# A selective-scan network on one core: two scan tiles per step in place of one

## Chip, core and metric

One core of a Trainium2 chip runs the whole program in one launch. The metric is the device time of that launch in microseconds (us). The engines are TensorE (PE, matmuls; PEld are its weight loads), VectorE (DVE), ScalarE (ACT), GpSimd (POOL) and SyncE (SP, which issues the DMAs here). Each engine works through its own queue in program order; semaphores make it wait for the others.

## What is computed

Four layers on four images of 64 x 64 positions (L = 4,096 tokens) and 96 channels. Layer 0 has a gated recurrence, layers 1 to 3 a convolution and a selective scan in four directions; each layer ends with a small quantised feed-forward part. The change is in the scan of layers 1 to 3. Cut to what matters, one of them is:

```python
xc = silu(depthwise_conv3x3(x @ in_proj) + conv_b)        # 192 channels
xs = [rows of xc, columns of xc, both flipped]            # 4 directions
dts, B, C = split(xs @ x_proj)                            # 6, 16 and 16 rows
delta = softplus(dts @ dt_proj + dt_bias)
dA = exp(delta[..., None] * A)                            # 16 states per channel
def step(h, t):
    h = dA_t * h + (delta_t * u_t)[..., None] * B_t       # the recurrence over L
    return h, einsum('bkdn,bkn->bkd', h, C_t)             # y: sum over the 16 states
y = scan(step) + D * xs
x = x + (layernorm(sum of the 4 directions of y) * silu(z)) @ out_proj
x = x + ffn(layernorm(x))
```

Everything around the recurrence (projections, convolution, norms, feed-forward) is the "side work" below.

## The kernel before

**Tiles.** The recurrence of one image and layer is cut into items: 2 flip directions (`d`) x 4 segments of T = 1,024 tokens x 3 chunks of 128 rows. A chunk holds 64 channels in row order and 64 in column order. An item has NS = 16 tiles, one for each state n, of 128 partitions x 1,024 tokens in float32. With 3 layers and 4 images there are 288 items and 4,608 tiles, numbered k = 16 q + n.

**What a tile costs.** Six helpers make a tile (lines 876 to 958):
- `c_rows(k)`: two DMAs on SP spread the state's row of C over the partitions into a buffer `c` (6 buffers).
- `decays(k)`: ACT makes `da = exp(delta * A_n)` (3 buffers).
- `b_rows(k)`: PE multiplies a selection matrix with the rows of B (`bs`, bfloat16 parts), two matmuls of 512 columns, into `bc` in PSUM. `wide()` (line 119) gives it one of 2 buffers of [128, 1024].
- `scan(k, beside)`: DVE multiplies `bc` by `du` (= delta * u) in place, the product; then `beside()` issues a portion of side work; then DVE runs `tensor_tensor_scan` over the 1,024 tokens into `h` (3 buffers), starting from the column `carry[:, n]`.
- `carry(k)`: ACT copies the last column of `h` into `carry` for the next segment. `times_c(k)`: POOL multiplies `h` by `c`, in place of `c`.
- `accumulate(k)`: PE adds the 16 tiles of an item up in PSUM (`acc`, one buffer of [128, 1024]) with eight 64 x 64 matmul instructions; the first tile of an item adds eight more for the skip term or the other direction's sum. `take` copies the full `acc` to SBUF on ACT and `store` sends it to DRAM in four DMAs.

**Order.** Nothing reorders the instructions of an engine: the class `InOrder` (line 68) chains every engine's instructions in the order in which the program text issues them, SP's DMAs too. So the loop over tiles (lines 990 to 1043) fixes all five queues. One turn k issues: `carry(k-1)`, `c_rows(k+2)`, `decays(k+2)`, `b_rows(k+1)`, `times_c(k-1)`, the product of k, side work, the scan of k, `accumulate(k-3)`. On DVE that is product, side work, scan, product, side work, scan and so on.

**Side work.** `beside()` advances generators by one `yield` each: `chain` prepares delta and du of the next item (`prepare_chunk`: two PE matmuls, ACT exponentials and logarithms, four POOL operations), `segment` the B and C rows of the next segment (`prepare_segment`), and `work()` steps a `Job` at a rate of 1.6 rounds a turn, which is the previous and the next image's norms, projections, convolution and feed-forward. Side work has 2 PSUM banks, counted by `bank`, `release` and `settle`. At n = 13 `beside` finishes the preparation of the next item. `logarithms()` issues ACT's collected logarithms at n = 11.

**PSUM.** 2 x 2 banks for `bc`, 2 for side work, 2 for `acc`: all 8 are used.

Of the kernel before, what the change touches and what calls it, by code (L numbers as in the profile page):

```python
# [15 lines left out]
ALU = mybir.AluOpType  # L16
# [5 lines left out]
NS = 16  # L22
# [3 lines left out]
T = 1024  # L26
# [73 lines left out]
def metaformer(ctx: ExitStack, tc: tile.TileContext, x, l0_ab, l0_rest, ssm, ffn, out):  # L100
# [10 lines left out]
    def sb(bufs, tag, shape, dtype=F32):  # L111
        return pools[bufs].tile(shape, dtype, tag=tag, name=tag)
# [19 lines left out]
    def settle():  # L132
        banks["free"] += banks["back"]
        banks["back"] = 0
# [38 lines left out]
    for n in range(NS):  # L173
        for k in range(2):
            at = NS * k + n
# [678 lines left out]
    def scans(stages, jobs, pac):  # L854


        items = [
            Item(im, layer, d, seg if d == 0 else NSEG - 1 - seg, chunk)
            for im, layer in stages
            for d in range(2)  # L860
            for seg in range(NSEG)
            for chunk in range(3)
        ]
        at = lambda q: items[q] if 0 <= q < len(items) else None
        sg = load_segment(items[0])
        for i in items[:3]:
            i.sg = sg
        drain(Chain(prepare_segment(items[0], sg), True))
        drain(Chain(prepare_chunk(items[0]), True))
        tiles = [(i, n) for i in items for n in range(NS)]  # L870
        last = len(tiles) - 1
        live = {}
        carries = {}
        per = 2 * NSEG * 3

        def start(i):
            if i.first:
                carries[i.chunk] = sb(2, f"carry{i.chunk}", [128, NS])
                pool.memset(carries[i.chunk], 0.0)
            i.carry = carries[i.chunk]  # L880

        def c_rows(k):
            i, n = tiles[k]
            c = live[k, "c"] = sb(6, "c", [128, T])
            for half in range(2):
                row = NS * half + n
                sp.dma_start(
                    out=c[64 * half : 64 * half + 64],
                    in_=i.sg.cs[row : row + 1, :].to_broadcast([64, T]),
                )  # L890

        def decays(k):
            i, n = tiles[k]
            da = live[k, "da"] = sb(3, "da", [128, T])
            at = (3 * i.d + i.chunk) * NS + n
            act.activation(da, i.delta, AF.Exp, scale=weights[i.layer].decay[:, at : at + 1])

        def b_rows(k):
            i, n = tiles[k]
            b = live[k, "b"] = wide()  # L900
            for half in range(2):
                cols = slice(half * MM, (half + 1) * MM)
                pe.matmul(
                    b[:, cols], sel[:, n, :], i.sg.bs[:, cols], start=True, stop=True
                )

        def scan(k, beside):
            i, n = tiles[k]
            da, b = live.pop((k, "da")), live.pop((k, "b"))
            dve.tensor_tensor(b, i.du, b, ALU.mult)  # L910
            beside()
            h = live[k, "h"] = sb(3, "h", [128, T])
            step = slice(None, None, -1 if i.d else 1)
            dve.tensor_tensor_scan(
                h[:, step],
                da[:, step],
                b[:, step],
                initial=i.carry[:, n : n + 1],
                op0=ALU.mult,
                op1=ALU.add,  # L920
            )

        def carry(k):
            i, n = tiles[k]
            if not i.last:
                end = 0 if i.d else T - 1
                act.copy(i.carry[:, n : n + 1], live[k, "h"][:, end : end + 1])

        def times_c(k):
            i, n = tiles[k]  # L930
            c = live[k, "c"]
            pool.tensor_tensor(c, live.pop((k, "h")), c, ALU.mult)

        def add_quarters(i, v, lhs, start, stop):

            for k in range(2):
                for j in range(2):
                    p = slice(64 * j, 64 * j + 64)
                    o = 64 * (j ^ k)
                    pe.matmul(  # L940
                        i.acc[o : o + 64, j * MM : (j + 1) * MM],
                        lhs[p],
                        v[p, k * MM : (k + 1) * MM],
                        start=start,
                        stop=stop,
                        tile_position=(64 * j, o),
                    )

        def accumulate(k):
            i, n = tiles[k]  # L950
            h = live.pop((k, "c"))
            if n == 0:
                i.acc = pac.tile([128, T], F32, tag="acc", name="acc")
                if i.d == 0:
                    add_quarters(i, i.sg.us[i.chunk], weights[i.layer].skip[:, i.chunk, :], True, False)
                else:
                    add_quarters(i, i.yf, stacked, True, False)
            add_quarters(i, h, stacked, False, n == NS - 1)

        def take(i):  # L960
            i.y = sb(2, "y", [128, T])
            act.copy(i.y, i.acc)

        def store(i):
            for j in range(2):
                for k in range(2):
                    o = 64 * (j ^ k)
                    t = i.seg * T + k * MM
                    sp.dma_start(
                        out=i.im.y[i.chunk, 64 * j : 64 * j + 64, t : t + MM],  # L970
                        in_=i.y[o : o + 64, j * MM : (j + 1) * MM],
                    )

        chain = segment = None
        start(items[0])
        c_rows(0)
        c_rows(1)
        decays(0)
        decays(1)
        b_rows(0)  # L980
        working = []

        def work():

            while working and working[0].done:
                working.pop(0)
            if working:
                working[0].step()

        for k in range(last + 5):  # L990
            q, n = divmod(k, NS)
            if k <= last:
                item = items[q]
                nxt = at(q + 1)
                if n == 0:
                    if q % per == 0:
                        item.im.y = dram.tile([3, 128, L], F32, tag="y", name="y")
                        working += jobs[q // per]
                    if item.chunk == 2:
                        drain(segment, work, lambda: nxt.sg.steps)  # L1000
                    chain = Chain(prepare_chunk(nxt), True) if nxt is not None else None
                if item.chunk == 1 and n == 4 and at(q + 2) is not None:
                    if q % per == per - 2:
                        for job in jobs[q // per][:1]:
                            while not job.done:
                                work()
                                settle()
                    segment = Chain(next_segment(items[q + 2 : q + 5]))
                if n == 8 and nxt is not None:
                    start(nxt)  # L1010
                if n == 8 and nxt is not None and nxt.d == 1:
                    nxt.yf = sb(2, "y", [128, T])
                    sp.dma_start(out=nxt.yf, in_=nxt.im.y[nxt.chunk, :, nxt.seg * T : (nxt.seg + 1) * T])
            def beside():
                pump(chain)
                pump(segment)
                if n == 13:
                    drain(chain, work)
                    if item.chunk == 2:
                        drain(segment, work)  # L1020
                work()

            full = items[(k - 4) // NS] if k >= 4 and (k - 4) % NS == NS - 1 else None
            if full is not None:
                take(full)
            if 0 <= k - 1 <= last:
                carry(k - 1)
            if k + 2 <= last:
                c_rows(k + 2)
                decays(k + 2)  # L1030
            if n == 11:
                logarithms()
            if k + 1 <= last:
                b_rows(k + 1)
            if 0 <= k - 1 <= last:
                times_c(k - 1)
            if k <= last:
                scan(k, beside)
            if full is not None:
                store(full)  # L1040
            if 0 <= k - 3 <= last:
                accumulate(k - 3)
            settle()
        while working:
            work()
            settle()
# [377 lines left out]
```

## Time and profile before

| | |
|---|---|
| median of 3 runs | 19,418.7 us (19,401.0 to 19,423.9) |
| span of the profiled execution | 19,402.3 us |
| layer 0 | 0 to about 1,800 us |
| scans of layers 1 to 3 | about 1,800 to 19,187 us |
| rest of the last image | 19,187 to 19,402 us |
| busy, whole span | DVE 17,697.8 us (91%), PE 15,935.0 (82%), POOL 15,479.3 (80%), ACT 12,105.6 (62%) |
| DMA | 3,192 MB, mean 165 GB/s, queue 1 busy 62.3% of 16 engines' span |

Almost every instruction is put down to line 78, the helper of `InOrder`, so that groups are told apart by the tiles that they write and read: `bc<-du,bc` on DVE is the product, `h<-da,carry,bc` the scan, `c<-h,c` on POOL is `times_c`, `bc<-bs,sel` on PE is `b_rows`, `acc<-c,twice` is `accumulate`. A matmul in float32 appears as two instructions. The granted clock is the share of its full speed that PE was allowed; the records show 1.0 and 0.5 only. A group's idle time is that of its engine just before its instructions, with the instruction that ended most of it.

In the 40 slices of the page VectorE is busy nine tenths or more from the fifth slice to the thirty-seventh:

```
PE   8998787787788788788788788788788787787887
DVE  6757999999999999999999999999999999999895
ACT  4544665665665665675665675665665665666665
POOL 3435888888888888888888888888888888888885
PEclk9998796786786797797797797797797797788775
```

### The profile page before, as it was taken

What the parts mean: (1) busy time and instruction counts of PE and PEld (TensorE: products, weight loads), DVE (VectorE), ACT (ScalarE), POOL (GpSimd) and SP (SyncE); (2) the same over time, 40 slices, a digit from 0 to 9 for tenths busy, and PEclk for the clock granted to TensorE, in tenths of its full rate; (3) what the DMA queues carried; (4) which work ended last, traced back from release to release, by engine and by line L of the source; (5) the groups of instructions that cost most, each with busy time, mean ns of one, the idle gap of its engine ahead of it and who ended that gap; (6) DMA issues with size and microseconds to landing.
All of it is one profiled execution on the core that took longest, in us unless ns stands there. A gap on an engine that the chain in (4) does not pass through costs nothing. (4 is left out here: it accounts for less than half of the span.)

```text
span 19402.3 us, 222370 instructions
## 1 busy us (share of the span) xinstructions
PE 15935.0 (82%) x69248; PEld 4652.0 (24%) x69248; DVE 17697.8 (91%) x13768; ACT 12105.6 (62%) x19150; POOL 15479.3 (80%) x10086
## 2 busy tenths in 40 slices
PE   8998787787788788788788788788788787787887
PEld 3332121121122222222222222222222222222323
DVE  6757999999999999999999999999999999999895
ACT  4544665665665665665675665665665665666665
POOL 3435888888888888888888888888888888888885
PEclk9998796786786797797797797797797797788775
DMA  2213666676676666666667676667676676676664
GB/s 53 50 46 87 166 187 172 167 191 168 167 190 173 173 183 182 172 183 181 172 187 183 172 186 178 170 185 185 170 191 177 170 192 175 171 193 170 168 180 115
DMA packets 1269866, 3192.20 MB, mean 165 GB/s; under 512 B 440336, under 2 KB 440560, under 8 KB 1262544
## 3 DMA queue, kind: packets, MB, share of 16 engines
q1 hardware_dynamic: 1268688, 3177.97, 62.3%
q8 instruction: 559, 9.16, 0.2%
q14 instruction: 619, 5.07, 0.1%
HBM read 2818.51 MB, written 308.28 MB: 161 GB/s over the span
## 5 line engine op out<-in xcount | busy, mean ns | idle before, releaser
L78 POOL TENSOR_TENSOR c<-h,c 128x1024 f32<-128x1024 f32 (+1 forms) x4992 | 11318.6, 2274 | 3241.4 <-DVE h L78 1326.1
L78 DVE TENSOR_TENSOR_SCAN h<-da,carry,bc 128x1024 f32<-128x1024 f32 x4608 | 10798.3, 2343 | 567.9 <-POOL c L78 63.3
L78 PE MATMUL acc<-c,twice 64*64 64x512 f32 x36864 | 6385.9, 770 | 39.2 <-POOL c L78 39.1
L78 ACT ACTIVATE da<-delta,decay 128x1024 f32<-128x1024 f32 x4608 | 5284.4, 1148 | 1425.8 <-DVE h L78 1414.0
L78 DVE TENSOR_TENSOR bc<-du,bc 128x1024 f32<-128x1024 f32 x4608 | 5569.1, 1209 | 287.4 <-PE bc L78 264.7
L78 PE MATMUL bc<-bs,sel 96*128 96x512 bf16 x9216 | 3486.1, 468 | 2663.6 <-DVE h L78 2562.1
L78 ACT COPY carry<-h 128x1 f32<-128x1 f32 x3456 | 649.0, 188 | 3121.5 <-DVE h L78 3117.1
L78 PEld LDWEIGHTS <-sel 96*128 96x128 bf16 x9216 | 561.9, 102 | 7786.2 <-DVE h L78 5970.8
L78 PEld LDWEIGHTS acc<-c,twice 64*64 64x64 f32 x36864 | 1148.5, 156 | 2882.6 <-issue 1988.2
L78 ACT ACT_TABLE_LOAD x1166 | 1496.0, 1283 | 36.8 <-DVE mv L78 20.2
L78 PE MATMUL conv<-pad,tap_lo 128*128 128x512 f32 x1728 | 919.9, 639 | 0.0
L78 PE MATMUL dt_proj<-rows,w 12*128 12x512 f32 x1152 | 846.8, 822 | 9.6 <-ACT delta L78 5.5
L78 ACT COPY y<-acc 128x1024 f32<-128x1024 f32 x288 | 291.5, 1012 | 822.6 <-PE acc L78 807.4
L78 PE MATMUL x_proj<-u,xp 128*108 128x512 f32 x1152 | 706.2, 731 | 31.4 <-ACT u L78 12.4
L78 POOL TENSOR_TENSOR delta<-delta,du 128x1024 f32<-128x1024 f32 x288 | 679.3, 2359 | 60.5 <-ACT du L78 58.9
L78 ACT ACTIVATE du<-e,ones 128x1024 f32<-128x1024 f32 x576 | 659.8, 1146 | 108.6 <-POOL delta L78 103.7
L78 POOL TENSOR_TENSOR e<-e,du 128x1024 f32<-128x1024 f32 x288 | 679.6, 2360 | 2.4 <-ACT du L78 2.4
L78 POOL TENSOR_TENSOR du<-delta,u 128x1024 f32<-128x1024 f32 x288 | 679.6, 2360 | 0.1
L78 ACT ACTIVATE c<-c,l_bias 128x512 f32<-128x512 f32 x384 | 263.4, 686 | 667.0 <-PE c L78 664.2
L78 POOL TENSOR_TENSOR delta<-delta,e 128x1024 f32<-128x1024 f32 x288 | 678.4, 2356 | 0.1
L78 PE MATMUL conv<-pad,tap_hi 128*128 128x512 f32 (+1 forms) x1152 | 609.0, 632 | 19.0 <-ACT u L78 16.7
L78 DVE TENSOR_TENSOR_SCAN h<-da,l_carry,bc 128x512 f32<-128x512 f32 x384 | 491.4, 1280 | 42.4 <-DVE bc L78 1.8
(149 smaller groups left out, 14606.8 us busy)
## 6 DMA issues: line engine op xcount, KB each, us to landing
c<-cs SPq DMA_DIRECT2D x9216, 256.0 KB, 4.2
u<-u SPq DMA_DIRECT2D x288, 512.0 KB, 6.7
y<-y SPq DMA_DIRECT2D x1152, 128.0 KB, 3.5
y<-y SPq DMA_DIRECT2D x144, 512.0 KB, 6.2
xr<-x SPq DMA_DIRECT2D x224, 192.0 KB, 5.0
u<-u SPq DMA_DIRECT2D x288, 128.0 KB, 3.8
pad<-y SPq DMA_DIRECT2D x288, 128.0 KB, 4.5
z<-zl SPq DMA_DIRECT2D x96, 256.0 KB, 4.4
```

The lines of the kernel that those rows point to most:

```text
L78: ins = f(*a, **k).ins
```

## The change

The loop takes two tiles a = 2j and b = 2j + 1 per step. `scan` is split into `times_b` (the product) and `scan`, and `beside` is called twice a step, with `settle` inside. The order of one step on each engine becomes:

- DVE: product a, side work, product b, scan a, side work, scan b.
- PE: accumulate a-4, accumulate b-4, side work, rows of a+2, side work, rows of b+2.
- ACT: decay of b, carry of a-2 and b-2, decay of a+2, side work twice; at step 1 of an item also `take` of the item before.
- POOL: `times_c` of b-2, side work twice, `times_c` of a.
- SP: `c_rows` of a+2 and b+2, each issued behind the accumulation that frees its buffer; side work's DMAs; `store`.

The instructions themselves, their number and their sizes stay, and so do the buffers. The reading of `live[k, "h"]` changes because `carry` now comes after `times_c` for tile a.

```diff
@@ -904,11 +904,14 @@
                     b[:, cols], sel[:, n, :], i.sg.bs[:, cols], start=True, stop=True
                 )
 
-        def scan(k, beside):
+        def times_b(k):
+            i, n = tiles[k]
+            b = live[k, "b"]
+            dve.tensor_tensor(b, i.du, b, ALU.mult)
+
+        def scan(k):
             i, n = tiles[k]
             da, b = live.pop((k, "da")), live.pop((k, "b"))
-            dve.tensor_tensor(b, i.du, b, ALU.mult)
-            beside()
             h = live[k, "h"] = sb(3, "h", [128, T])
             step = slice(None, None, -1 if i.d else 1)
             dve.tensor_tensor_scan(
@@ -929,7 +932,7 @@
         def times_c(k):
             i, n = tiles[k]
             c = live[k, "c"]
-            pool.tensor_tensor(c, live.pop((k, "h")), c, ALU.mult)
+            pool.tensor_tensor(c, live[k, "h"], c, ALU.mult)
 
         def add_quarters(i, v, lhs, start, stop):
 
@@ -973,11 +976,10 @@
 
         chain = segment = None
         start(items[0])
-        c_rows(0)
-        c_rows(1)
+        for k in range(2):
+            c_rows(k)
+            b_rows(k)
         decays(0)
-        decays(1)
-        b_rows(0)
         working = []
 
         def work():
@@ -987,31 +989,36 @@
             if working:
                 working[0].step()
 
-        for k in range(last + 5):
-            q, n = divmod(k, NS)
-            if k <= last:
+        half = NS // 2
+        for j in range(len(tiles) // 2 + 2):
+            q, m = divmod(j, half)
+            a, b = 2 * j, 2 * j + 1
+            on = b <= last
+            if on:
                 item = items[q]
                 nxt = at(q + 1)
-                if n == 0:
+                if m == 0:
                     if q % per == 0:
                         item.im.y = dram.tile([3, 128, L], F32, tag="y", name="y")
                         working += jobs[q // per]
                     if item.chunk == 2:
                         drain(segment, work, lambda: nxt.sg.steps)
                     chain = Chain(prepare_chunk(nxt), True) if nxt is not None else None
-                if item.chunk == 1 and n == 4 and at(q + 2) is not None:
+                if item.chunk == 1 and m == 2 and at(q + 2) is not None:
                     if q % per == per - 2:
                         for job in jobs[q // per][:1]:
                             while not job.done:
                                 work()
                                 settle()
                     segment = Chain(next_segment(items[q + 2 : q + 5]))
-                if n == 8 and nxt is not None:
+                if m == 4 and nxt is not None:
                     start(nxt)
-                if n == 8 and nxt is not None and nxt.d == 1:
-                    nxt.yf = sb(2, "y", [128, T])
-                    sp.dma_start(out=nxt.yf, in_=nxt.im.y[nxt.chunk, :, nxt.seg * T : (nxt.seg + 1) * T])
-            def beside():
+                    if nxt.d == 1:
+                        nxt.yf = sb(2, "y", [128, T])
+                        t = slice(nxt.seg * T, (nxt.seg + 1) * T)
+                        sp.dma_start(out=nxt.yf, in_=nxt.im.y[nxt.chunk, :, t])
+
+            def beside(n):
                 pump(chain)
                 pump(segment)
                 if n == 13:
@@ -1019,28 +1026,42 @@
                     if item.chunk == 2:
                         drain(segment, work)
                 work()
-
-            full = items[(k - 4) // NS] if k >= 4 and (k - 4) % NS == NS - 1 else None
-            if full is not None:
-                take(full)
-            if 0 <= k - 1 <= last:
-                carry(k - 1)
-            if k + 2 <= last:
-                c_rows(k + 2)
-                decays(k + 2)
-            if n == 11:
+                settle()
+
+            if on:
+                decays(b)
+            for k in (a - 2, b - 2):
+                if 0 <= k <= last:
+                    carry(k)
+            if a + 2 <= last:
+                decays(a + 2)
+            if m == 5:
                 logarithms()
-            if k + 1 <= last:
-                b_rows(k + 1)
-            if 0 <= k - 1 <= last:
-                times_c(k - 1)
-            if k <= last:
-                scan(k, beside)
-            if full is not None:
-                store(full)
-            if 0 <= k - 3 <= last:
-                accumulate(k - 3)
-            settle()
+            if 0 <= b - 2 <= last:
+                times_c(b - 2)
+                del live[a - 2, "h"], live[b - 2, "h"]
+            for k in (a - 4, b - 4):
+                if 0 <= k <= last:
+                    accumulate(k)
+                if k + 6 <= last:
+                    c_rows(k + 6)
+            if on:
+                times_b(a)
+            beside(2 * m)
+            if on:
+                times_b(b)
+                scan(a)
+            if a + 2 <= last:
+                b_rows(a + 2)
+            beside(2 * m + 1)
+            if on:
+                times_c(a)
+                scan(b)
+            if b + 2 <= last:
+                b_rows(b + 2)
+            if m == 1 and q >= 1:
+                take(items[q - 1])
+                store(items[q - 1])
         while working:
             work()
             settle()
```

## The prediction

> **What bounds the kernel now.** I read the page first, its groups of instructions before the rest. Columns: instruction, written tile, read tiles, count; busy us and mean ns of one; idle time before them and what ended it.
>
> ```profile
> L78 DVE TENSOR_TENSOR_SCAN h<-da,carry,bc 128x1024 f32<-128x1024 f32 x4608 | 10798.3, 2343 | 567.9 <-POOL c L78 63.3
> L78 PE MATMUL acc<-c,twice 64*64 64x512 f32 x36864 | 6385.9, 770 | 39.2 <-POOL c L78 39.1
> L78 DVE TENSOR_TENSOR bc<-du,bc 128x1024 f32<-128x1024 f32 x4608 | 5569.1, 1209 | 287.4 <-PE bc L78 264.7
> L78 PE MATMUL bc<-bs,sel 96*128 96x512 bf16 x9216 | 3486.1, 468 | 2663.6 <-DVE h L78 2562.1
> ```
>
> VectorE makes 4,608 products of 1.209 us and 4,608 scans of 2.343 us. They run from 1,800 to 19,187 us, so I took the busy time of that stretch (columns: PE, PE loads, DVE, ACT, POOL in us and instructions, granted clock, DMA share, GB/s).
>
> ```profile
> 1800.00:19187.00 17387.00, 14190.06 (x64226) 3923.56 (x64226) 16498.10 (x11920) 11172.77 (x17204) 14719.51 (x8759) 0.79 0.67 177
> ```
>
> VectorE is busy 16,498 of 17,387 us, 95%; POOL 85%, PE 82% at a mean clock of 0.79, ACT 64%. VectorE sets the pace, 3.773 us a tile, and PE and POOL are not far behind. The timeline of VectorE shows where its remaining idle time is (start, duration).
>
> ```profile
> 8028.06 2.35 DVE L78 TENSOR_TENSOR_SCAN h<-da,carry,bc 128x1024 f32<-128x1024 f32 x1
> 8030.32 1.21 DVE L78 TENSOR_TENSOR bc<-du,bc 128x1024 f32<-128x1024 f32 x1
> 8031.66 2.35 DVE L78 TENSOR_TENSOR_SCAN h<-da,carry,bc 128x1024 f32<-128x1024 f32 x1
> 8033.93 1.21 DVE L78 TENSOR_TENSOR bc<-du,bc 128x1024 f32<-128x1024 f32 x1
> ```
>
> A product that needs nothing of the scan ahead of it starts 2.26 us after that scan's start, before its 2.35 us are over. A scan that reads the product just ahead starts 1.34 us after it, 0.13 us behind its end. The records of all tiles say the same: median -84 ns at scan to product, +134 ns at product to scan where nothing lies between.
>
> **What the change takes away.** In the new order (product a, side work, product b, scan a, side work, scan b) no scan follows its own product directly. Each such place gives back 134 + 84 = 218 ns. They are found from the scan's row: 567.9 us idle less some 80 us that are waits, over 134 ns, is about 3,640 tiles; counted in the trace, 3,709 have no VectorE instruction between. The other 899 have side work there and already start 80 ns early; they gain nothing. 3,709 x 0.218 = **809 us**. The number and the size of products and scans stay.
>
> [...]
>
> **What it adds: PE's row matmuls come late.** A product reads `bc`, which PE fills with two matmuls (`b_rows`). There are two such buffers, so tile k+2's rows wait for tile k's scan. Before, `b_rows(k+1)` starts when scan k-1 ends and product k+1 runs after product k and scan k, 3.6 us later; the rows take 0.6 to 1.03 us, so 2.5 us or more are spare. The waits of VectorE show how seldom that fails (us in total, times, longest):
>
> ```profile
> DVE bc L78 <- PE bc L78: 264.7, 232, 6.3
> ...
> DVE h L78 <- POOL c L78: 63.9, 31, 13.4
> ```
>
> Now lay out a new step without VectorE side work, time 0 at the end of the scan before: product a to 1.12 us, product b to 2.25, scan a to 4.51, scan b to 6.77 (pitches 1.209 and 2.343 less 0.085). PE's order in a step is two accumulations, side work, rows of the next a, side work, rows of the next b. Its durations depend on the granted clock, 1.0 for 58% of the scans' stretch and 0.5 for 42%:
>
> ```profile
> 8012.47 1.03 PE L78 MATMUL bc<-bs,sel 96*128 96x512 bf16 x2 [2.09 <-DVE h L78]
> ...
> 8015.53 1.98 PE L78 MATMUL acc<-c,twice 64*64 64x512 f32 x8
> ...
> 8029.35 1.09 PE L78 MATMUL acc<-c,twice 64*64 64x512 f32 x8
> 8030.46 0.60 PE L78 MATMUL bc<-bs,sel 96*128 96x512 bf16 x2
> ```
>
> Rows of b can't start before scan b ends. With 0.05 us to see it and 0.04 us until VectorE sees the result they are ready 0.69 us (full clock) or 1.12 us (half) later; product b wants them at 1.12. Spare: 0.43 us or none, and that only if PE has finished the second side work, which it begins when the rows of a are done, 4.56 + 0.61 = 5.17 us (5.60). So this side work may last 2.0 us at full clock and 1.15 us at half before VectorE stands still. Rows of a have to start by 6.12 us (5.69); ahead of them lie rows 0.66 (1.08) and two accumulations 2.18 (3.97), which leaves 3.2 us (0.6) for the first side work.
>
> I summed PE's side work between the rows of one tile and the next over the trace: 2,900 of 4,608 places have some, 867 over 2 us. Of the second places, 1,535 ran at full clock, 218 over 2.0 us, 193 us in excess; 769 at half, 222 over 1.15, 220 us. Of the first places, 70 at full clock exceed 3.2 us by 36 us and 492 at half exceed 0.6 us by 603 us. Together **1,052 us**; scaled to full clock throughout, 246 us. These take the place of the 265 us shown, which fall away. Between the ends I take 950, near the recorded clock, because the clock is steady, 0.76 from 1,800 to 6,000 us and 0.80 in each stretch of 4 ms after that.
>
> The clock's records step in 3.41 us. Taken with PE's busy time, a stretch at 1.0 ends after a step that was 46% busy on average, one at 0.5 after a step 99% busy. The new order gives PE one half step with both accumulations and one with rows and side work alone, so half-empty windows stay. [...]
>
> **Side work.** PE's side matmuls also wait for ACT, POOL and DVE: the twelve largest such rows of its waits (`in_xt`, `y_c`, `ff_y`, `ff_xt` and so on) add up to 452 us. Now hidden by the spare 2.5 us, they delay rows in the second place, that is for half of them: 226 us; bounds 0 and 452. `take` moves behind the side work of step 1 of an item, ahead of the next item's first accumulation: 288 copies of 1.01 us, 291 us at most; PE has 3.2 us there at full clock, so 0, with 291 kept as a bound.
>
> **At nothing.** `c_rows` now waits on SP's queue for accumulation k-6 and `store` for `take`, with the next rows' DMAs queued behind; used about 11 us after issue against 4.2 us to landing; without that cover POOL's 271 us of waits on c would grow by the same lateness. `decays(b)` is issued in its own step, 4.5 us ahead of scan b, 1.15 us long; VectorE waits 11 us for it today. `carry` runs twice in a row on ACT, 0.19 us each. `h` has three buffers: scan b needs the product on POOL of tile b-3, which may now lag 4.4 us instead of 6.2; the row above (63.9 us) is the lower bound, and the second rival the upper. `settle` inside the side work and `logarithms` at step 5 move no work.
>
> **Sum.** -809 - 265 + 950 + 226 = +102 us. On the profiled span of 19,402.3 us: 19,504. The median of the runs, 19,418.7, is 16 us above the span: **19,520 us**, 0.5% slower.
>
> **Rivals.** *The clock rises.* PE does the same work in less time, falls below half busy more seldom, and the late rows cost 246 us: -809 - 265 + 246 + 113 (half of the side term) = -715, 18,700; halfway, 19,110. It decides from a granted clock of about 0.85 on: late rows must cost less than 809 + 265 - 226 - 39 = 809 us, and on the line from 1,052 us at 0.79 to 246 us at 1.0 that is 0.853. For it: PE is 99% busy before each return to full. Against: PE at 0.79 for the whole stretch.
>
> *POOL becomes the bound.* It has 14,720 us of work in the stretch. Its product of tile a is queued behind both side works, and these wait for ACT and PE. If each of the 2,304 steps lost another 0.3 us to it, +690: 20,210. Against it: 64 us of such waits today and 2,667 us of idle time.
>
> *The gap stays.* If the 134 ns were no dependence but belonged to every product, nothing comes back: 19,520 + 809 = 20,330. Against it: with side work between, scans start 80 ns early.
>
> **How the numbers follow.** The forecast, rows late about as much as the gap gives back (19,330 to 19,950): 0.53. The clock or better slack carrying much of the gain through (18,600 to 19,330): 0.35. POOL as the bound: 0.07. The gap stays: 0.05. A change counts as measurable from 0.2%, 39 us, that is below 19,380 or above 19,458. Of the forecast's share 0.03 falls below and 0.10 between. So faster 0.38, no difference 0.10, slower 0.52. The forecast's own range is 19,330 to 19,950. Leaving out the lowest third of the faster case and half of the two slowest, 18,900 to 20,050 holds 8 in 10.
>
> **What would show it.** Scans that start 2.26 us after a scan's start and none at +134 ns: the gain. Waits of the product for `bc` at some 900 to 1,200 us instead of 265, mostly at tile b: the loss; below 400 with a clock over 0.85, the first rival is right. Waits of scans for POOL above 500 us would be the second. I am wrong in sign if PE's side work is better covered by VectorE's side work in the same place than I counted, which was not at all.

## The result and the profile after

The changed kernel takes 19,585 us (median of 4 runs, 19,562 to 19,604) against 19,419 before: 1.009 times as long, interval 1.0075 to 1.0104. Forecast were 19,520 us and a chance of 0.52 for slower. The profiled execution has a span of 19,560.2 us, 157.9 more than before; the scans of layers 1 to 3 take 17,542 us instead of 17,387, so practically all of it lies there.

First the timeline of VectorE in the changed kernel (start, duration, count of merged instructions):

```profile
8022.85 0.41 DVE L78 BATCH_NORM_STATS2 st<-xh 128x6 f32<-128x96 f32 x2
8023.18 0.36 DVE L78 BATCH_NORM_AGGREGATE mv<-st 128x2 f32<-128x6 f32 x4
8023.45 1.21 DVE L78 TENSOR_TENSOR bc<-du,bc 128x1024 f32<-128x1024 f32 x1
8024.57 4.57 DVE L78 TENSOR_TENSOR_SCAN h<-da,carry,bc 128x1024 f32<-128x1024 f32 x2
8029.06 2.33 DVE L78 TENSOR_TENSOR bc<-du,bc 128x1024 f32<-128x1024 f32 x2
8031.30 2.34 DVE L78 TENSOR_TENSOR_SCAN h<-da,carry,bc 128x1024 f32<-128x1024 f32 x1
8034.80 2.35 DVE L78 TENSOR_TENSOR_SCAN h<-da,carry,bc 128x1024 f32<-128x1024 f32 x1 [1.16 <-POOL c L78]
```

Product b at 8,023.45 lasts 1.21 us and scan a starts at 8,024.57, before the product ends: the gap of 0.13 us is gone. Two scans take 4.57 us, less than twice 2.35. What came instead stands in the last row: a scan that waits 1.16 us for POOL. The page's groups (mean ns of one; idle time before and its main cause) and VectorE's waits (us in total, times, longest) show all of it:

```profile
L78 DVE TENSOR_TENSOR_SCAN h<-da,carry,bc 128x1024 f32<-128x1024 f32 x4608 | 10613.5, 2333 | 330.5 <-POOL c L78 203.1
...
L78 DVE TENSOR_TENSOR bc<-du,bc 128x1024 f32<-128x1024 f32 x4608 | 5521.2, 1216 | 812.1 <-PE bc L78 783.4
```

```profile
DVE bc L78 <- PE bc L78: 783.4, 642, 16.1
...
DVE h L78 <- POOL c L78: 203.5, 115, 7.7
DVE h L78 <- ACT carry L78: 90.2, 56, 3.9
...
DVE st L78 <- DMA xr<-x: 74.3, 22, 6.6
DVE x L78 <- PE out_proj L78: 56.9, 27, 7.4
```

The scan's idle time fell from 568 to 331 us, the product's rose from 287 to 812. The mean clock of TensorE in the stretch from 1,800 to 19,187 us is 0.81 (0.79 before):

```profile
1800.00:19187.00 17387.00, 13601.31 (x63714) 4151.52 (x63714) 16094.21 (x11828) 10956.23 (x17072) 14551.84 (x8704) 0.81 0.70 176
```

For an account of all the runs I charge each VectorE instruction of the scans with the time by which it starts later than 85 ns ahead of the end of the one before it, which is how an instruction starts that nothing holds back. The charge is put down to what ended the wait; "gap" is the charge of about 218 ns of a scan behind its own product. `xr` (a DMA) and `out_proj` (matmuls) are waits of VectorE's side work. "All" is the sum over every instruction, with the smaller charges that have no column and with starts still earlier than 85 ns counted as gains. In us:

| | gap | product a for `bc` | product b for `bc` | scan for POOL | scan for carry | scan for `da` | `xr` | `out_proj` | all | scans' stretch |
|---|---|---|---|---|---|---|---|---|---|---|
| before | 761 | 124 | 164 | 66 | 0 | 13 | 14 | 4 | 1,274 | 17,387 |
| changed | 0 | 260 | 589 | 218 | 95 | 25 | 76 | 44 | 1,446 | 17,542 |

(In the kernel before, a and b are the even and the odd tiles.) The gap's 761 us came back and 933 us of other charges came, of which 561 us for rows of B. Products take 7 ns longer, scans 10 ns less: together -12 us, side work -4.

### The profile page after: what moved, and what is told of

It is laid out like the page before. It is cut to its first block, busy times and chain, and to the rows that moved or that the text cites. A ratio compares the mean times of both kernels' runs of the same rounds, so it can differ in the third digit from the quotient of the medians.

```text
span 19560.2 us, 226829 instructions
## 1 busy us (share of the span) xinstructions
PE 15455.9 (79%) x69248; PEld 4904.9 (25%) x69248; DVE 17451.8 (89%) x13768; ACT 11957.0 (61%) x19082; POOL 15438.8 (79%) x10086
## 5 line engine op out<-in xcount | busy, mean ns | idle before, releaser
L78 DVE TENSOR_TENSOR_SCAN h<-da,carry,bc 128x1024 f32<-128x1024 f32 x4608 | 10613.5, 2333 | 330.5 <-POOL c L78 203.1
L78 PE MATMUL acc<-c,twice 64*64 64x512 f32 x36864 | 6093.6, 790 | 2.6 <-POOL c L78 2.6
L78 PE MATMUL bc<-bs,sel 96*128 96x512 bf16 x9216 | 3297.5, 447 | 3463.5 <-DVE h L78 3403.8
L78 PEld LDWEIGHTS acc<-c,twice 64*64 64x64 f32 x36864 | 1532.1, 171 | 3433.5 <-issue 2833.2
L78 PEld LDWEIGHTS <-sel 96*128 96x128 bf16 x9216 | 632.6, 102 | 6375.0 <-DVE h L78 5667.9
L78 ACT ACTIVATE e<-dt_proj,w 128x512 f32<-128x512 f32 x576 | 394.3, 684 | 1295.0 <-PE dt_proj L78 1294.8
L78 ACT COPY carry<-h 128x1 f32<-128x1 f32 x3456 | 539.3, 185 | 846.4 <-DVE h L78 844.6
L78 PE MATMUL dt_proj<-rows,w 12*128 12x512 f32 x1152 | 762.5, 745 | 1.3 <-DVE rows L78 1.3
```

Of the source, the lines that this page charges most:

```text
L78: ins = f(*a, **k).ins
```

## The experiments

All ratios are to the kernel before in runs on the same chip. Times are medians. The kernel before took 19,407 to 19,419 us in these sets of runs; the changed kernel was not run again in them, so a difference from its 19,585 us is uncertain by some 10 us beyond the spread of its own runs.

**Product b back behind scan a.**

```diff
-                times_b(b)
                 scan(a)
             if a + 2 <= last:
                 b_rows(a + 2)
+            if on:
+                times_b(b)
             beside(2 * m + 1)
```

> One part undone: on VectorE the product of b goes back behind scan a, so that each product stands right ahead of its own scan again (unless side work lies between); the other engines keep the new order. If the gap between a product and its scan is a real dependence and the rows of B are what the change pays, about 3,700 gaps of 219 ns come back (+809 us) while the rows of b gain 2.26 us of slack, so that most of the 589 us that the product of b loses to them goes: 19,750 to 19,900 us. If the gap was never worth its 809 us in the new order, or the losses lie elsewhere (POOL, ACT), the time stays within 100 us of the changed kernel's 19,585 or the waits of the product for bc stay above 700 us.

Measured: 19,779 us, ratio 1.0186 (1.0169 to 1.0203). The gap is back with 753 us, product b waits 77 us for its rows instead of 589, product a 265, all charges 1,673.

```profile
DVE bc L78 <- PE bc L78: 310.3, 274, 12.8
...
DVE h L78 <- POOL c L78: 143.7, 92, 5.8
```

The scan's idle time on the page, 331 us in the changed kernel, is back at 743:

```profile
L78 DVE TENSOR_TENSOR_SCAN h<-da,carry,bc 128x1024 f32<-128x1024 f32 x4608 | 10796.7, 2343 | 743.2 <-POOL c L78 143.0
```

The time is inside the expected 19,750 to 19,900 us, and both halves of the theory hold: the gap is worth its 753 us, and removing it takes away the slack of product b's rows, at 512 us. The net 194 us is what the new order on VectorE gains; the new order of the other engines costs more than that, as this run is some 360 us above the kernel before.

**Half of the accumulation.**

```diff
-            add_quarters(i, h, stacked, False, n == NS - 1)
+            if n % 2 == 0 or n == NS - 1:
+                add_quarters(i, h, stacked, False, n == NS - 1)
```

> Leaves out the accumulation of the odd tiles of an item except the last (7 of 16), so the sum over states is incomplete and TensorE has about 1.2 us less to do per step of two tiles, all of it ahead of the rows of a. If TensorE's load ahead of the rows is what makes products late, the product of a waits for bc less than 100 us (260 in the changed kernel), product b about the same 500 to 600, the time falls to 19,250 to 19,450 us. If the granted clock matters more than the load, the emptier TensorE is granted less (below 0.78 against 0.818), the product of b waits longer, and the time stays within 100 us of 19,585. If rows are not the loss, no wait of the product for bc changes.

Measured: 19,648 us, 1.0119 (1.0104 to 1.0134), slower than the changed kernel. Product a waits 193 us, product b 730. The windows view has the reason in its clock column, 0.69:

```profile
1800.00:19187.00 17387.00, 12869.56 (x47550) 3713.79 (x47551) 16049.08 (x11777) 10913.03 (x16979) 14474.20 (x8651) 0.69 0.69 175
```

TensorE has less to do and is granted less, as the second branch of the expectation had it. The first place (product a) gains a little from the lighter load. In the second the load did not change, but the clock did: sorted by the granted clock at their start, 1,351 of 2,304 rows of b ran at half clock (838 in the changed kernel), and product b's waits for such rows were 424 us (239).

**Second side work last.**

```diff
-            beside(2 * m + 1)
             if on:
                 times_c(a)
                 scan(b)
             if b + 2 <= last:
                 b_rows(b + 2)
+            beside(2 * m + 1)
```

> Moves the second portion of side work of every engine behind scan b and the rows of b+2, so VectorE runs product a, side work, product b, scan a, scan b, side work, and TensorE has nothing between the rows of a+2 and of b+2. If the second place is where the rows of b become late, the product of b waits for bc below 150 us instead of 589; the first place now carries both portions, and from the durations of the trace before the excess there is 517 us (full clock) and 936 us (half clock), so the product of a waits 700 to 1,400 us instead of 260, and the time is 19,700 to 20,400 us. If the rows are late because of the clock alone, or for a reason that has nothing to do with the place of the side work, the sum of both waits stays near 850 us and the time within 100 us of 19,585.

Measured: 19,628 us, 1.0112 (1.0097 to 1.0127). Product b no longer waits for rows to any amount that shows among the larger charges; product a waits 708 us, the low end of what was expected. The time is below the expected 19,700 to 20,400 us and within the 100 us that were given for the case that the place has no bearing; the waits decide for the first case all the same, as product b's went below the 150 us named for it. Scans wait 330 us for the carry. ACT's own order is that of the changed kernel, with two portions of side work ahead of the carry in both; ahead of the late carries, these portions waited 173 us for TensorE and 145 us for POOL in this trace. That the later place of the side work on the other engines causes this is argued, not shown.

```profile
DVE bc L78 <- PE bc L78: 655.5, 484, 8.5
DVE h L78 <- ACT carry L78: 313.7, 189, 4.3
```

So the place of TensorE's side work decides which product is late. Moved from one place to the other the loss stays nearly whole.

**Product in SBUF.**

```diff
-            b = live[k, "b"]
-            dve.tensor_tensor(b, i.du, b, ALU.mult)
+            b = live.pop((k, "b"))
+            h = live[k, "h"] = sb(4, "h", [128, T])
+            dve.tensor_tensor(h, i.du, b, ALU.mult)
...
-                b[:, step],
+                h[:, step],
```

> The changed kernel with the product written to the h buffer in SBUF and the scan run in place there, so the PSUM buffer of the rows is free after the product and no longer after the scan; h has four buffers, paid for by single buffers of ff_h and ff_h2 and two small tiles that share others. If the rows' wait for the scan is what the change pays, the waits of the product for bc fall from 783 us below 100 and the time to 18,700 to 18,950 us. A rival: a scan that reads both operands from SBUF while POOL works there is slower than 2.33 us, or POOL's products are slower than 2.36 us; 0.2 us on each scan would be +920 us, and the time 19,600 or more. A second rival: h buffers are now taken at the product, 2.3 to 4.5 us earlier, and VectorE waits for POOL instead, 300 us or more.

Measured: 26,114 us, 1.3453 (1.3433 to 1.3473). The tile's view (count; shortest, median and longest in ns):

```profile
L78 POOL TENSOR_TENSOR c<-h,c x4992: 1261/2363/6898, 58.4 to 25898.5; 128x1024 f32<-128x1024 f32 x184, 128x512 f32<-128x512 f32 x16
L78 DVE TENSOR_TENSOR h<-du,bc x4608: 1177/1195/1232, 1809.7 to 25888.6; 128x1024 f32<-128x1024 f32 x192
L78 DVE TENSOR_TENSOR_SCAN h<-da,carry,h x4608: 2310/4248/11943, 1812.0 to 25894.1; 128x1024 f32<-128x1024 f32 x192
```

The first rival, and far beyond its 0.2 us: a scan with both operands in SBUF takes 2.31 us at the least and 4.25 in the median; POOL's products reach 6.9 us (2.43 at the most in the changed kernel). The slow scans are those beside POOL: 2,945 with POOL busy all the while took 4.36 us in the median, and 16 with POOL idle 2.33 to 2.35, so the scan in place and in SBUF is not slow by itself. The product with one operand in PSUM is not touched (1.20 us in the median, 1.21 in the changed kernel). Product b still waits 308 us for rows, as TensorE was held up behind POOL (2,104 us of its accumulations' waits), so this run does not price the rows' wait for the scan. The second rival came too: products wait 384 us for POOL to free a buffer of `h`. It has a fourth buffer of `h`, paid for by single buffers of `ff_h` and `ff_h2`.

**Noughts for TensorE where there is no side work.** `fill(k, parts)` adds matmuls with zero weights to `acc`.

```diff
+            had = pe.n
             beside(2 * m)
+            if on and pe.n == had:
+                fill(b - 4, 2)
...
+            had = pe.n
             beside(2 * m + 1)
+            if on and pe.n == had:
+                fill(b - 4, 1)
```

> The changed kernel with more work for TensorE: where a portion of side work issues no matmul, TensorE adds noughts to acc (the weights are zero, so the result stays), eight 64x64 matmul instructions in the first place of a step, four in the second. If the granted clock is what makes the rows late, as the run with half the accumulation suggests (clock 0.713, waits of product b up from 589 to 730 us), the clock rises from 0.818 to above 0.90, the waits of the product for bc fall from 849 us (both tiles, counted against a start 85 ns early) to 250 to 500, and the time to 19,150 to 19,400 us. If it is TensorE's load, the added matmuls make it worse: waits above 1,000 us, time 19,750 us or more.

Measured: 19,455 us, 1.0025 (1.0013 to 1.0036), 130 us less than the changed kernel. The clock rose, though not above 0.90 (0.88 in the scans' stretch, 0.884 over the span); product a waits 189 us, but product b 610, no less than in the changed kernel. The expected 250 to 500 us of waits and 19,150 to 19,400 us were missed. (The helper is one line further down in this kernel, hence L79.)

```profile
1800.00:19187.00 17387.00, 14198.34 (x73334) 4385.72 (x73334) 16177.49 (x11891) 11028.69 (x17126) 14664.84 (x8746) 0.88 0.70 177
```

```profile
DVE bc L79 <- PE bc L79: 725.5, 675, 12.4
```

More work for TensorE made the kernel faster, so the clock counts; but in this form it is worth 130 us, not the bulk of product b's wait. The added matmuls hold rows up themselves: at the 1,583 tiles with noughts ahead of their rows the waits for rows rose from 13 us in the changed kernel to 80, and at all others they fell from 771 to 646. In the changed kernel's trace 240 of the 549 us that product b waited fall on 94 steps in which TensorE stood idle for over 0.3 us inside the second side work, waiting for a DMA, POOL or ACT; the same sort gives 241 us in this run.

**Carry and the product with C first.**

```diff
+            if 0 <= a - 2 <= last:
+                carry(a - 2)
             if on:
                 decays(b)
-            for k in (a - 2, b - 2):
-                if 0 <= k <= last:
-                    carry(k)
+            if 0 <= b - 2 <= last:
+                carry(b - 2)
...
+            if on:
+                times_c(a)
             beside(2 * m + 1)
             if on:
-                times_c(a)
                 scan(b)
```

> The changed kernel with two small moves: on ACT the carry of tile a-2 stands ahead of the decay of b, and on POOL the product of h and c of tile a stands ahead of the second portion of side work. If scans wait for h buffers because of these two orders (218 us for POOL, 95 us for the carry in the changed kernel), these waits fall below 120 us together and the time by 100 to 250 us, to 19,330 to 19,490. If POOL is late for want of throughput, the same waits come back elsewhere (side work on POOL later, ACT and TensorE behind it), and the time stays within 60 us of 19,585.

Measured: 19,696 us, 1.0145 (1.013 to 1.016): 111 us slower than the changed kernel. Waits for POOL and the carry fell from 313 to 154 us, and others came:

```profile
DVE bc L78 <- PE bc L78: 892.5, 716, 15.2
DVE h L78 <- ACT da L78: 173.6, 105, 3.5
```

Side work on POOL came later and ACT's behind it (ACT's waits for POOL's `norm` ahead of `xh` rose from 364 to 531 us), then TensorE's (`in_xt` for `xh`, 30 to 76 us), and the decay and the rows came late too. That chain fits the rival of the expectation, but no run takes it apart; the time went beyond the 60 us of the rival.

**Both edits together**, noughts and the two moves, with no other change.

> Both edits together: noughts added where there is no side work on TensorE, carry of a-2 and the product of h and c of a moved ahead. If the clock and the h buffers are separate losses, the gains of the two kernels with one edit each add up: 18,950 to 19,250 us, faster than the kernel before. If one covers the other, it is no better than the better of the two.

Measured: 19,558 us, 1.0075 (1.006 to 1.009), far from the expected 18,950 to 19,250. The two edits add up, 130 us gained and 111 lost against 27 us gained in all, but the second has the wrong sign.

**Noughts in the kernel before.** The same `fill` with one part per tile.

> The kernel before, with four 64x64 matmul instructions of noughts per tile where the side work issues no matmul. It has 265 us of waits of the product for bc and the gap of 134 ns behind 3,700 products. If a higher clock is worth something only where rows are late, it gains 100 to 200 us at most (19,220 to 19,320), with the clock above 0.88 instead of 0.80, and the gaps stay. If the clock has no bearing, 19,400 to 19,450.

Measured: 19,369 us, 0.9979 (0.9969 to 0.9988). The clock reached 0.911, the gap stayed (764 us), rows 271 us instead of 288:

```profile
DVE bc L79 <- PE bc L79: 252.0, 189, 5.9
```

In this kernel, where rows are early, a higher clock (0.911 in place of 0.80), with the load of the added matmuls, bought 38 us. That is less than the expected 100 to 200, though clear of the 19,400 us given for a clock without bearing.

**Rows of C at the end of the step.**

```diff
                 if 0 <= k <= last:
                     accumulate(k)
-                if k + 6 <= last:
-                    c_rows(k + 6)
...
+            for k in (a + 2, b + 2):
+                if k <= last:
+                    c_rows(k)
```

> The changed kernel with the C rows of a+2 and b+2 issued at the end of the step instead of behind the accumulations at its start. In the changed kernel SP holds the DMAs of the side work behind rows of C that wait for an accumulation: VectorE waits 74 us for xr (13 before) and TensorE 53 us for u (2 before). If SP's order costs that, xr falls below 25 us, u below 10, the product of b waits some 50 us less, and the time is 19,440 to 19,540 us. If the rows of C then land too late, POOL waits for c more than the 148 us of the changed kernel and the time is 19,600 us or more.

SP's timeline in the changed kernel shows the queue: six DMAs for rows of C hold SP for 9.75 us, and the side work's follow.

```profile
8010.02 9.75 SPq L78 DMA_DIRECT2D c<-cs  x6
8019.87 0.53 SPq L78 DMA_DIRECT2D x<-xh  x1
8020.45 1.79 SPq L78 DMA_DIRECT2D pad<-y  x3
8024.33 2.79 SPq L78 DMA_DIRECT2D c<-cs  x4
```

Measured: 19,417 us, 1.0003 (0.9993 to 1.0012), 168 us less than the changed kernel and more than expected. VectorE's waits of this run:

```profile
DVE bc L78 <- PE bc L78: 657.7, 599, 5.9
...
DVE h L78 <- POOL c L78: 246.7, 139, 15.1
...
DVE st L78 <- DMA xr<-x: 11.4, 7, 2.4
```

`xr` fell from 74 to 11 us, and TensorE's 53 us of waits for `u` no longer occur. Product b's charge fell from 589 to 454, more than the 50 us expected: a late DMA of the side work had held TensorE ahead of the rows. The sort by idle steps bears this out: of the 240 us in the changed kernel some 100 are left, and TensorE's idle time for DMAs in those steps fell from 88 to 2 us. The longest wait for rows is 5.9 us instead of 16.1.

The other branch of the expectation came as well, at a smaller price: POOL waits longer for rows of C (the changed kernel, then this run), and scans for POOL 263 us instead of 218.

```profile
POOL c L78 <- DMA c<-cs: 148.2, 34, 12.1
...
POOL c L78 <- DMA c<-cs: 229.7, 65, 15.1
```

**Both: rows of C last, and noughts.**

> The same with the noughts added where side work gives TensorE nothing to do (19,455 us without the move of the C rows). If the two are separate, 19,310 to 19,420 us, about the kernel before or a little faster; if the waits on SP's queue cover each other, 19,430 to 19,480.

Measured: 19,276 us, 0.9929 (0.9915 to 0.9944): the fastest of all, 0.7% under the kernel before and 1.6% under the changed one, and a little better than expected.

```profile
DVE bc L79 <- PE bc L79: 579.1, 602, 6.0
...
DVE h L79 <- POOL c L79: 218.7, 122, 14.3
```

**Statistics spread in the kernel before**, by itself and with noughts.

```diff
                 dve.bn_stats(st[:, g, :], src[:, g, 0:width])
-                if g % 2:
+                if g % 2 or spread:
                     yield
...
                 dve.bn_aggr(mv[:, g, :], st[:, g, :])
+                if spread and g < G - 1:
+                    yield
...
-                jobs[-1].append(Job(between(im, layer - 1), 1.6))
+                jobs[-1].append(Job(between(im, layer - 1), 1.7))
```

> The kernel before with the statistics of a norm (four bn_stats, four bn_aggr) issued one per portion of side work instead of two and four at a time, the job's rate 1.7 instead of 1.6. VectorE's instructions are the same; more of the 3,709 tiles without one between product and scan get one, and up to 219 ns of it is hidden there. By the rows (bn_stats 246 to 347 ns, bn_aggr 153 ns, each less 85 ns of overlap) 150 to 250 us of VectorE's side work can be hidden that is not hidden now: 19,170 to 19,270 us. If the gap were not filled by any independent instruction, or the finer portions make the jobs late, 19,400 us or more.

> The kernel before with both: statistics one per portion, and noughts for TensorE where the side work issues no matmul (0.998 of the kernel before by itself). If they add up, 19,130 to 19,230 us, the fastest of all; otherwise no better than the better of the two.

Measured: 19,715 us, 1.0159 (1.0144 to 1.0174), and 19,650 us, 1.0125 (1.0109 to 1.0141). Both missed. The gap fell as it should, from 761 to 644 us, but rows of B cost 445 us instead of 288, and the scans' stretch begins 95 us later and leaves 20 us more behind it, presumably because the side work that runs alone there takes more turns:

```profile
DVE bc L78 <- PE bc L78: 416.7, 274, 6.2
```

The finer portions change where all engines' side work falls, and the higher rate packs it more densely. Which of the two made the rows late was not told apart.

The account of these runs in us, as in the table above:

| | gap | product a | product b | scan for POOL | carry | `da` | `xr` | `out_proj` | all | stretch |
|---|---|---|---|---|---|---|---|---|---|---|
| product b behind scan a | 753 | 265 | 77 | 151 | 72 | 26 | 76 | 73 | 1,673 | 17,777 |
| half accumulated | 0 | 193 | 730 | 218 | 84 | 24 | 49 | 51 | 1,532 | 17,624 |
| second side last | 0 | 708 | - | 127 | 330 | 36 | 54 | 91 | 1,520 | 17,604 |
| noughts | 0 | 189 | 610 | 198 | 98 | 13 | 62 | 53 | 1,324 | 17,428 |
| carry and C first | 0 | 299 | 671 | 106 | 48 | 184 | 77 | 70 | 1,579 | 17,687 |
| rows of C last | 0 | 269 | 454 | 263 | 103 | 25 | 12 | 35 | 1,300 | 17,403 |
| rows of C last, noughts | 0 | 200 | 444 | 233 | 101 | 10 | 10 | 41 | 1,163 | 17,261 |

("-": not among the larger charges.)

## Why the prediction was right

**The gap, -809 us.** Right, and 48 us too large: of the 3,709 tiles 3,482 carry the plain gap, 761 us; none is left in the changed kernel, and the run that puts product b back returns 753. Two kinds of start stand in these traces: products and scans that don't depend on the one ahead start 84 to 92 ns before its end, a scan that reads the product just ahead 134 ns behind it.

**Late rows, +950 in place of 265, and +226 for waits inside the side work.** The mechanism was right and the size too large. Gross, 1,176 us were forecast for rows; 849 were charged. The term that was mis-sized is the first place: 639 us were worked out for it and 260 measured. For the second, 413 us and the 226 for waits inside the side work were forecast, 639 together, and 589 measured. In the first place the excess at half clock (603 us) was overestimated: product a's waits for rows that ran at half clock are 107 us in the changed kernel. The sum took each step's clock as it was recorded before; in the new order TensorE stays at half clock for 6.4 us on average instead of 11.8. That this is why the 603 us did not come is argued, not shown.

**The clock.** It went from 0.80 to 0.818. The first rival's line, from 1,052 us at 0.79 to 246 at full clock, is too steep: raising the clock to 0.884 took 50 us off the rows (849 to 799), where the line gives some 250 for the step from 0.818 to 0.884. Even without the 67 us by which waits rose where the matmuls were added, it is 125. The rival would not have decided at 0.85. Steps of 3.41 us ahead of a fall to 0.5 were 45% busy on average in the changed kernel, and 5 of its 1,027 falls in the scans' stretch followed a step without any matmul. The mean clock there followed the load: 0.81 in the changed kernel, 0.69 with half of the accumulation and 0.88 with noughts.

**What was put at nothing.** This is the part that failed. Scans wait 152 us more for POOL and 95 more for the carry; the three buffers of `h` were given as a bound of the forecast, but entered the sum with nothing, and the carry was given 0.19 us each without asking what stands ahead of it on ACT. `c_rows` on SP's queue was held to be covered by 11 us of lead. That holds for the rows of C themselves: POOL's waits for them fell from 271 to 148 us. It does not hold for what is queued behind: the side work's DMAs, whose lateness reached VectorE (`xr`, 74 us) and TensorE (`u`, 53 us) and through it the rows. The prediction did say that the next rows' DMAs queue behind, but priced POOL's waits for rows of C and not those of the side work. Moving the rows of C gives 168 us back. SP's own waits for accumulations did not grow (9,060 us against 9,450 before); why what stands behind them came later than before was not taken apart.

**Sum.** Forecast +102 us on the span, measured +158. Too much for rows (by 327 us) and too little for waits put at nothing (372 us in all, smaller rows included) nearly cancelled. The sign and the time were right for the right chief reason; that the size came so close is partly the luck of this cancelling. POOL as the bound and the gap that stays, the two slow rivals, did not come.

Open: how the 309 us of product b's wait that don't fall on idle steps divide between long side work and late rows of a; and what the rows' wait for the scan alone costs, which the SBUF run could not show.

## What to carry to other kernels

Taking a dependence off the engine that sets the pace gave back its gap here (753 to 761 us of 809 expected), but a reorder also moves the moment at which buffers come free: work out for each producer how long it has between that moment and its consumer, and what lies ahead of it in its own queue, before counting the gap as won. In SP's queue, kept in order here, rows of C that waited delayed the DMAs behind them (VectorE waited 74 us for `xr`, 13 before and 11 with the rows of C last), so price the DMAs behind one that waits, not only its own lead. TensorE with less to do was granted less here, 0.713 in place of 0.818 with half of the accumulation; in the kernels before and after, 98% of the 3.41 us steps at full clock in which it was less than half busy were followed by half the clock.

## What the runs showed of the hardware that was not expected

- A VectorE scan of 1,024 float32 elements took 2.33 us with its second operand in PSUM and 4.25 us in the median (2.31 at the least) with both in SBUF beside POOL's products, which took as much as 6.9 us (2.43 in the changed kernel).
- Removing 7 of 16 accumulations took the granted clock of TensorE from 0.818 to 0.713 and made the kernel slower by 63 us; adding matmuls of noughts took it to 0.884 and made it faster by 130 us.
- Two scans back to back start 2.26 us apart, as a scan and a product do.
